# Local attention on one core: mask added by a matmul, one minimum per head, exps from PSUM, and the rotary swap in one instruction

## The chip, the cores and the metric

The kernel runs on one core of a Trainium2 chip. Its engines work side by side, each through its own queue in order: TensorE (PE, with PEld for its weight loads), VectorE (DVE), ScalarE (ACT), GpSimd (POOL) and SyncE (SP, which issues most DMAs). Matmul results land in PSUM, which has eight banks of 128 partitions x 512 float32; other tiles lie in SBUF. The metric is device time of one execution in microseconds, taken as the median of several runs.

## The reference

The program is a chain of four attention layers, each followed by a feed-forward layer, with a residual sum and a layer norm after each, on an input of 4 x 512 rows of 128 numbers as the kernel sees it. The change is in the second of these eight stages, a small transformer of two layers with local attention: 8 heads of 64 numbers, windows of 64 rows, and each row sees its own window up to itself and the window before. Cut to what matters:

```python
q, k = l2norm(q) * qs, l2norm(k) * ksc
q, k = rotary_xpos(q, k)          # q*cos*scale + rotate_half(q)*sin*scale
bq = q.reshape(b, h, w, 64, d) * 8.0
bk, bv = look_around(bk), look_around(bv)      # window before and own: 128 keys
sim = einsum('bhwid,bhwjd->bhwij', bq, bk)
mask = (i < j) | (i > j + 64) | (j == -1)
attn = softmax(where(mask, -max, sim))
out = einsum('bhwij,bhwjd->bhwid', attn, bv)
```

## The kernel before

**Units and heads.** Class F0 holds the stage. A unit u is one layer and one block of 512 rows: two layers x four blocks are 8 units. A unit has 8 heads, taken in 4 pairs, so there are 64 heads and 32 pairs. `run` goes over the heads as items. For each item it writes: the scores of a pair (every second item), `score` of the head, `turn` of the head four items back, and then some steps of the generators that run beside it: `qkv` of the next unit, `values` (the product with V), and `post` of the unit before (projection, layer norm, gated feed-forward).

**What sets the order.** The functions write instructions one after another with a rising priority number. A scheduler then lays out each engine's queue: of the instructions whose inputs and buffers it holds to be ready it takes the one with the lowest number. `k.front()` lowers the number of the score matmuls by 400, so they are laid out as early as their banks allow. `k.waits` adds a wait by hand.

**Scores.** `scores` takes the two PSUM banks with the tag "s", one for each head of the pair. Into each go 16 matmuls of 64 keys' depth: for each window w a 64 x 128 piece (64 query rows, 128 keys). A bank thus holds a head's 512 query rows as four chunks c of 128 rows x 128 keys. The signs in the rotary table make the scores negative, so that the softmax's maximum is a minimum here. There are only two such banks, so the next pair's matmuls cannot start until the readers of this pair are done; the first also waits by hand for `self.emptied`, which is the last reader of the second head.

**Softmax.** In `score`, for each chunk, VectorE adds the mask (`band`, 0 or 1e20) to the scores, multiplies by the inverse norm of the query row (`rn`), writes the result to the SBUF tile `sm` (one buffer) and its row minimum to `nb`, all in one instruction (L1689). ScalarE then reads `sm`, computes exp(nb - sm) into `p`, and gives the row sum to `den` (L1691). `turn` transposes `p` on TensorE (L219) and copies it to `PT` (L1701).

**Rotary.** In `qkv`, for q and k of each chunk, ScalarE copies the projection from PSUM (L1616) and squares it (L1619); VectorE multiplies the swapped halves of each head by the sine table into `tb` (L1623, twice: one instruction for each half), the straight values by the cosine table in place (L1625), and sums the squares (L1626).

**Other names.** L311 to L313 are the three matmuls of a projection in split precision; L1653 scales k by its norm; L343 to L353 are small VectorE steps of an inverse square root; L1726 is the copy of a pair's output; L1333 is a row minimum of another stage (A3), read from a PSUM bank; L1996 and L2117 are ScalarE instructions of other stages, without and with a per-partition scale; L725 is a mask matmul of another stage.

Of the kernel before, what the change touches and what calls it, by code (L numbers as in the profile page):

```python
# [452 lines left out]
class Attn:  # L453
# [4 lines left out]
    nb, lead, lag, ahead = 3, 8, 5, 2  # L458
# [333 lines left out]
class Alibi(Causal):  # L792
    MROW, alibi, nm = 30, True, "a2"
    nb, lead, pre, span = 4, 12, True, "first"
# [18 lines left out]
class Rel(Attn):  # L813
# [4 lines left out]
    nb, lead, lag, ahead = 3, 6, 4, 3  # L818
# [674 lines left out]
class F0:  # L1493
# [83 lines left out]
    def qkv(self, u, X, tag="t"):  # L1577
# [5 lines left out]
        w = self.w  # L1583
# [20 lines left out]
        for c in range(4):  # L1604
            cs = slice(c * P, (c + 1) * P)
            for s in range(3):
                yield from wait()
                ps = k.bank("b")
                ws = slice(512 * s, 512 * s + 512)
                k.mm3(ps, xh[:, cs], xl[:, cs], w["qkvh"][:, ws], w["qkvl"][:, ws])  # L1610
                if s == 2:
                    nc.scalar.copy(v[:, c, :], ps)
                    yield
                    continue
                x = kr[:, c, :] if s else pool.tile([P, 512], F32, tag="ta", name=f"ta{u}{c}", bufs=self.nta)
                nc.scalar.copy(x, ps)  # L1616
                yield
                sq = pool.tile([P, 512], F32, tag="sq", name=f"sq{u}{c}{s}", bufs=1)
                nc.scalar.activation(sq, x, AF.Square)  # L1619
                tb = pool.tile([P, 8, 64], F32, tag="tb", name=f"tb{u}{c}{s}", bufs=2)  # L1620
                x3 = x.rearrange("p (h d) -> p h d", d=64)
                for a, b2 in ((0, 32), (32, 0)):
                    nc.vector.tensor_tensor(tb[:, :, a:a + 32], x3[:, :, b2:b2 + 32],  # L1623
                                            w["tab"][:, 2 * s + 1, c, None, a:a + 32].to_broadcast([P, 8, 32]), ALU.mult)
                nc.vector.tensor_tensor(x3, x3, w["tab"][:, 2 * s, c, None, :].to_broadcast([P, 8, 64]), ALU.mult)  # L1625
                nc.vector.tensor_reduce(ss[:, s, c, :], sq.rearrange("p (h d) -> p h d", d=64), AX.X, ALU.add)  # L1626
# [36 lines left out]
    def scores(self, u, pr):  # L1663


        k, nc = self.k, self.nc
        qT, kT = self.S[u][:2]
        if pr == 0:
            self.den[u] = self.early.tile([P, 4, 8], F32, tag="den", name=f"den{u}", bufs=2)
        self.s = [k.bank("s") for _ in range(2)]  # L1670
        with k.front():
            for w in range(8):
                c, o = w // 2, 64 * (w % 2)
                for e in range(2):
                    r = slice(64 * e, 64 * e + 64)
                    m = nc.tensor.matmul(self.s[e][o:o + 64, c * P:c * P + P], qT[r, pr, 64 * w:64 * w + 64], kT[r, pr, 64 * w:64 * w + P], start=True, stop=True)  # L1676
                    if w == e == 0 and self.emptied:
                        k.waits(m.ins, self.emptied)

    def score(self, u, h):  # L1680

        k, nc, pool = self.k, self.nc, self.pool
        rn, den, s = self.S[u][3], self.den[u], self.s[h % 2]
        p = self.p[8 * u + h] = pool.tile([P, 4, P], F32, tag="p", name=f"p{u}{h}", bufs=self.np)
        nb = pool.tile([P, 4], F32, tag="nb", name=f"nb{u}{h}", bufs=3)
        sm = pool.tile([P, 4, P], F32, tag="sm", name=f"sm{u}{h}", bufs=self.ns)
        for c in range(4):

            m = nc.vector.tensor_tensor_reduce(sm[:, c, :], s[:, c * P:c * P + P], self.band[:, min(c, 1), :],  # L1689
                                           rn[:, 0, c, h:h + 1], 3.0e38, ALU.add, ALU.min, nb[:, c:c + 1])  # L1690
            nc.scalar.activation(p[:, c, :], sm[:, c, :], AF.Exp, bias=nb[:, c:c + 1], scale=-1.0, accum_out=den[:, c, h:h + 1])  # L1691
        self.emptied = m.ins

    def turn(self, u, h):
# [149 lines left out]
    def run(self, Xs):  # L1844
# [4 lines left out]
        self.sel = self.early.tile([P, 4, P], F32R, name="f0sel")  # L1849
        self.lT = k.rows16(self.early, "f0lT")  # L1850
        nc.gpsimd.dma_start(self.sel, k.d["c_sel8"])
        self.v2 = pool.tile([P, 4, 512], F32, name="f0v2")
        nc.gpsimd.memset(self.v2[0:64, 0:1], 0.0)
        self.p, self.emptied = {}, None
# [536 lines left out]
```

## Time and profile before

| | |
|---|---|
| three runs | 2244.31, 2245.49, 2246.03 us; median 2245.49 |
| the profiled execution's own time | 2249.67 us |
| its span, first to last instruction | 2247.6 us |
| mean granted TensorE clock in it | 0.965 |
| stretch in which the attention of the changed stage runs | from 247.7 us (first L1689) to 634.2 us (last L1691) |
| instructions in the span | 43130 |

A profile shows one execution. Busy time is the time in which an engine works; matmuls overlap and their ends are modelled, so a busy TensorE is not one at its peak. A group's row gives line, engine, operation, what it writes and reads, shapes and count; after the first bar stand busy us in all and the mean ns of one; after the second the idle time of the engine just before, and what ended most of it. A wait's row gives who waited for whom: us in all, times, longest. The chain of waits is followed back from the last instruction, at each step to what released it or to the instruction before it on its engine.

### The profile page before, as it was taken

The page shows a single profiled execution, that of the slowest core. Times are in us where ns is not written, and L with a number is a line of the kernel's source. Part 1 is how long each engine was busy: PE and PEld are TensorE (multiplying, and loading weights), DVE is VectorE, ACT ScalarE, POOL GpSimd, SP SyncE. Part 2 cuts the span into 40 slices and gives each one's busy share as a digit, 9 for nine tenths or more (in the row PEclk, how much of TensorE's full clock was granted, in tenths as well). Part 3 has the DMA queues.
Part 4 walks back from the last instruction along what each step waited for, and adds up shares of the span by engine and source line. Part 5 has one row for each costly group of instructions (what it writes and reads, how often), then busy time and mean ns, then how long its engine had stood idle before and what let it go on. Part 6 is the DMA issues. An engine that isn't in the chain of part 4 may idle for free.

```text
span 2247.6 us, 43130 instructions
## 1 busy us (share of the span) xinstructions
PE 2025.6 (90%) x14400; PEld 1472.7 (66%) x14400; DVE 1669.2 (74%) x5592; ACT 1331.7 (59%) x2982; POOL 504.3 (22%) x707
## 2 busy tenths in 40 slices
PE   7999888888878999999999999998999899999897
PEld 4566566676656667676887665776666566666676
DVE  5778688888878676873777775553877877778787
ACT  3566787777734666665333666332877777777632
POOL 3222212111211532433000322531111111111220
PEclk9999999999988999999999999998999999999999
DMA  5321312021433454321021420603889888888400
GB/s 170 106 77 35 102 49 62 8 48 27 116 113 94 143 157 140 113 79 56 16 66 40 117 78 21 218 17 90 209 213 210 203 196 190 195 206 204 104 5 15
DMA packets 264919, 242.10 MB, mean 108 GB/s; under 512 B 106353, under 2 KB 190619, under 8 KB 263867
## 3 DMA queue, kind: packets, MB, share of 16 engines
q1 hardware_dynamic: 259466, 221.86, 37.0%
q0 software_dynamic: 5232, 17.50, 3.3%
q8 instruction: 115, 1.88, 0.4%
q14 instruction: 106, 0.86, 0.1%
HBM read 103.82 MB, written 74.32 MB: 79 GB/s over the span
## 4 chain that ended last, share of the span: by engine, by line
PE 59%; DVE 17%; ACT 9%; DMA 7%; issue 4%; POOL 2%; SPq 1%; ACTq 0%; POOLq 0%; DVEq 0%
PE t L219 5%; PE s L2113 4%; PE o L737 3%; PE s L688 3%; PE t L721 3%; PE o L1377 3%; PE o L1016 3%; PE b L219 3%; PE b L311 3%; PE o L2009 2%; PE s L311 2%; PE b L313 2%; PE b L312 2%; PE s L313 2%; PE s L312 2%
## 5 line engine op out<-in xcount | busy, mean ns | idle before, releaser
L969 DVE CUSTOM_DVE_ANT_0 junk<-w,a1mask 128x640 bf16<-128x640 f32 x256 | 202.9, 817 | 66.3 <-PE w L967 64.4
L219 PE MATMUL t<-ident,p 128*128 128x128 f32 x1280 | 200.6, 278 | 26.4 <-ACT p L1334 17.3
L765 ACT ACTIVATE Pt<-t 128x384 f32<-128x384 f32 (+1 forms) x384 | 179.6, 528 | 67.4 <-PE t L721 55.7
L219 PEld LDWEIGHTS t<-ident,p 128*128 128x128 f32 x1280 | 151.2, 141 | 83.5 <-ACT p L1334 38.3
L1347 ACT COPY PT<-t 128x512 f32<-128x512 f32 x256 | 149.9, 595 | 76.2 <-PE t L219 75.3
L1043 ACT ACTIVATE Pt<-t 128x512 f32<-128x512 f32 x256 | 149.1, 597 | 73.4 <-PE t L1042 44.4
L1334 ACT ACTIVATE p<-s,nb 128x512 f32<-128x512 f32 x256 | 178.2, 700 | 12.4 <-DVE nb L1333 6.7
L1333 DVE TENSOR_REDUCE nb<-s 128x1 f32<-128x512 f32 x256 | 174.4, 685 | 2.5
L690 DVE CUSTOM_DVE_ANT_0 junk<-s,a0mask 128x128 bf16<-128x128 f32 (+3 forms) x256 | 114.1, 484 | 45.9 <-PE s L688 45.0
L1352 DVE CUSTOM_DVE_ANT_0 jk<-p,a3right 128x496 bf16<-128x496 f32 (+3 forms) x256 | 124.6, 487 | 26.9 <-ACT p L1334 14.8
L690 DVE CUSTOM_DVE_ANT_0 junk<-s,a2mask 128x128 bf16<-128x128 f32 (+3 forms) x256 | 114.8, 483 | 30.5 <-PE s L688 30.4
L774 POOL TENSOR_SCALAR_AFFINE_SELECT Pt<-Pt 128x512 f32<-128x512 f32 x112 | 70.0, 637 | 256.4 <-ACT Pt L765 256.3
L1331 DVE TENSOR_TENSOR s<-s,W 128x160 f32<-128x160 f32 (+1 forms) x256 | 80.9, 317 | 62.5 <-PE s L1329 61.2
L1328 PE MATMUL s<-a3KT,a3QT 128*128 128x512 f32 x256 | 118.7, 466 | 5.6 <-DVE nb L1333 2.5
L1377 PE MATMUL o<-PT,V 128*64 128x512 f32 x512 | 116.9, 598 | 0.5 <-ACT PT L1347 0.5
L1691 ACT ACTIVATE p<-sm,nb 128x128 f32<-128x128 f32 x256 | 100.7, 397 | 24.8 <-DVE nb L1689 24.4
L1329 PE MATMUL s<-a3K,a3Q 128*128 128x512 f32 x256 | 102.1, 400 | 0.0
L1040 PE MATMUL t<-a1Q,a1K 128*128 128x512 f32 (+3 forms) x256 | 92.4, 366 | 6.3 <-ACT Pt L1043 3.9
L1689 DVE CUSTOM_DVE_ANT_0 sm<-s,band,rn 128x128 f32<-128x128 f32 x256 | 78.2, 343 | 26.4 <-PE s L1676 19.3
L688 PE MATMUL s<-a0K,a0Q 128*128 128x256 f32 (+2 forms) x256 | 83.8, 387 | 14.4 <-DVE mx L690 7.3
L966 PE MATMUL w<-a1K,a1Q 128*128 128x256 f32 (+2 forms) x192 | 83.1, 433 | 10.6 <-DVE mx L969 9.7
L1996 ACT ACTIVATE sl<-s 128x512 f32<-128x512 f32 x64 | 37.9, 598 | 91.0 <-PE s L313 85.6
(493 smaller groups left out, 5803.3 us busy)
## 6 DMA issues: line engine op xcount, KB each, us to landing
W<-a3dsk SPq DMA_DIRECT2D x32, 640.0 KB
a1Q<-a1iq SPq DMA_DIRECT2D x32, 512.0 KB
a3dpw<-p SPq DMA_DIRECT2D x64, 160.0 KB
a3dpw<-p SPq DMA_DIRECT2D x64, 144.0 KB
a1K<-a1ik SPq DMA_DIRECT2D x64, 128.0 KB
a3Q<-a3dim SPq DMA_DIRECT2D x32, 256.0 KB
a3QT<-H SPq DMA_DIRECT2D x64, 128.0 KB
a3QT<-L SPq DMA_DIRECT2D x64, 128.0 KB
```

Source lines behind the costliest of these rows:

```text
L219: return self.nc.tensor.matmul(out.bitcast(x.dtype), x, i[:n, :n], is_transpose=True, start=start, stop=stop)
L688: self.scored = nc.tensor.matmul(s[:, :nm], self.qof(0, t, i)[:, qc * P:(qc + 1) * P], Ks[:, i, :nm], start=True, stop=True).ins
L690: nc.vector.tensor_tensor_reduce(junk[:, :n], s[:, :n], k.mask[:, 512 - n:512], 1.0, NEG, ALU.add, ALU.max, mx[:, qc, i:i + 1])
L765: ready = nc.scalar.activation(Pt[:, i, z:], s[:, z:], AF.Exp, scale=sc).ins
L969: nc.vector.tensor_tensor_reduce(junk, s.rearrange("p a n -> p (a n)")[:, T - n:T + m], k.mask[:, T - n:T + m], 1.0, NEG, ALU.add, ALU.max ...
L1043: nc.scalar.activation(Pt[:, i, :T], s, AF.Exp, scale=sc)
L1328: nc.tensor.matmul(s, QT[:, e, qs], KT[:, e, :], start=True, stop=False)
L1333: nc.vector.tensor_reduce(nb, s, AX.X, ALU.min)
L1334: nc.scalar.activation(p[:, e, :], s, AF.Exp, bias=nb, scale=-1.0, accum_out=den[:, qc, 2 * un + e:2 * un + e + 1])
L1347: self.copied[t] = nc.scalar.copy(PT[e][:, :, qc * P:qc * P + P], tb.rearrange("p (c n) -> p c n", n=P)).ins
L1352: nc.vector.tensor_tensor_reduce(jk[:, :nn], p[:, e, x0:], w["right"][:, :nn], 1.0, 0.0, ALU.mult, ALU.add, at[:, e, qc, 31:32])
L1377: m = nc.tensor.matmul(o[64 * e:64 * e + 64, :], V[:, kc, h * 64:h * 64 + 64], PT[e][:, kc, :], start=(kc == 0), stop=False)
```

## The change

Four things change. The mask is added inside the scores' bank: a matmul of a bfloat16 identity with a bfloat16 copy of the mask for all four chunks (`band4`) opens each bank, and the score matmuls accumulate on it. VectorE takes the minimum of all four chunks in one reduction over the bank and multiplies the four results by the norm. The exps read the scores from PSUM, with the negated norm (`mrn`, made once per unit) as their scale and the scaled minimum as their bias, so `sm` is gone, and `emptied` is now an exp. Apart from that, the two instructions of the rotary swap become one that walks the halves in reverse. The identity and the mask copies are made once, when the stage starts.

```diff
@@ qkv
-                for a, b2 in ((0, 32), (32, 0)):
-                    nc.vector.tensor_tensor(tb[:, :, a:a + 32], x3[:, :, b2:b2 + 32],
-                                            w["tab"][:, 2 * s + 1, c, None, a:a + 32].to_broadcast([P, 8, 32]), ALU.mult)
+                nc.vector.tensor_tensor(tb.rearrange("p h (a d) -> p h a d", a=2), x.rearrange("p (h a d) -> p h a d", a=2, d=32)[:, :, ::-1],
+                                        w["tab"][:, 2 * s + 1, c].rearrange("p (a d) -> p a d", a=2)[:, None].to_broadcast([P, 8, 2, 32]), ALU.mult)
@@ scores
         if pr == 0:
+            self.mrn = self.pool.tile([P, 4, 8], F32, tag="mrn", name=f"mrn{u}", bufs=2)
+            nc.vector.tensor_scalar(self.mrn, self.S[u][3][:, 0], -1.0, None, ALU.mult)
             self.den[u] = ...
         self.s = [k.bank("s") for _ in range(2)]
         with k.front():
+            for e in range(2):
+                m = nc.tensor.matmul(self.s[e], self.identb, self.band4.rearrange("p c n -> p (c n)"), start=True, stop=False)
+                if e == 0 and self.emptied:
+                    k.waits(m.ins, self.emptied)
             for w in range(8):
                 c, o = w // 2, 64 * (w % 2)
                 for e in range(2):
                     r = slice(64 * e, 64 * e + 64)
-                    m = nc.tensor.matmul(self.s[e][o:o + 64, c * P:c * P + P], qT[...], kT[...], start=True, stop=True)
-                    if w == e == 0 and self.emptied:
-                        k.waits(m.ins, self.emptied)
+                    nc.tensor.matmul(self.s[e][o:o + 64, c * P:c * P + P], qT[...], kT[...], start=False, stop=(w >= 6))
@@ score
-        nb = pool.tile([P, 4], F32, tag="nb", name=f"nb{u}{h}", bufs=3)
-        sm = pool.tile([P, 4, P], F32, tag="sm", name=f"sm{u}{h}", bufs=self.ns)
-        for c in range(4):
-            m = nc.vector.tensor_tensor_reduce(sm[:, c, :], s[:, c * P:c * P + P], self.band[:, min(c, 1), :],
-                                           rn[:, 0, c, h:h + 1], 3.0e38, ALU.add, ALU.min, nb[:, c:c + 1])
-            nc.scalar.activation(p[:, c, :], sm[:, c, :], AF.Exp, bias=nb[:, c:c + 1], scale=-1.0, accum_out=den[:, c, h:h + 1])
+        nb = pool.tile([P, 2, 4], F32, tag="nb", name=f"nb{u}{h}", bufs=3)
+        nc.vector.tensor_reduce(nb[:, 0], s.rearrange("p (c n) -> p c n", n=P), AX.X, ALU.min)
+        nc.vector.tensor_tensor(nb[:, 1], nb[:, 0], rn[:, 0, :, h], ALU.mult)
+        for c in range(4):
+            m = nc.scalar.activation(p[:, c, :], s[:, c * P:c * P + P], AF.Exp, bias=nb[:, 1, c:c + 1], scale=mrn[:, c, h:h + 1],
+                                     accum_out=den[:, c, h:h + 1])
         self.emptied = m.ins
@@ run
+        self.identb = pool.tile([P, P], BF16, name="f0identb")
+        nc.vector.tensor_copy(self.identb, k.ident)
+        self.band4 = pool.tile([P, 4, P], BF16, name="f0band4")
+        nc.vector.tensor_copy(self.band4[:, 0], self.band[:, 0])
+        nc.vector.tensor_copy(self.band4[:, 1:], self.band[:, 1, None].to_broadcast([P, 3, P]))
```

More of the change, by code (lines that the diff above doesn't have):

```diff
@@ L1675, in scores @@
                     r = slice(64 * e, 64 * e + 64)
[L1676 to L1678 removed]
+                    nc.tensor.matmul(self.s[e][o:o + 64, c * P:c * P + P], qT[r, pr, 64 * w:64 * w + 64], kT[r, pr, 64 * w:64 * w + P], start=False, stop=(w >= 6))
     def score(self, u, h):
         k, nc, pool = self.k, self.nc, self.pool
[L1683 removed]
+        rn, mrn, den, s = self.S[u][3], self.mrn, self.den[u], self.s[h % 2]
         p = self.p[8 * u + h] = pool.tile([P, 4, P], F32, tag="p", name=f"p{u}{h}", bufs=self.np)
[L1685 to L1686 removed]
+        nb = pool.tile([P, 2, 4], F32, tag="nb", name=f"nb{u}{h}", bufs=3)
+        nc.vector.tensor_reduce(nb[:, 0], s.rearrange("p (c n) -> p c n", n=P), AX.X, ALU.min)
+        nc.vector.tensor_tensor(nb[:, 1], nb[:, 0], rn[:, 0, :, h], ALU.mult)
         for c in range(4):
[L1689 to L1691 removed]
+            m = nc.scalar.activation(p[:, c, :], s[:, c * P:c * P + P], AF.Exp, bias=nb[:, 1, c:c + 1], scale=mrn[:, c, h:h + 1],
+                                     accum_out=den[:, c, h:h + 1])
         self.emptied = m.ins
```

## The prediction

> **What bounds the kernel now.** I read the page's first part, then cut out the stretch in which the changed lines run (247 to 640 us), and there the busy times, the chain of waits, the groups, the waits and a few rows in order of time.
>
> Over the whole span TensorE looks like the bound:
>
> ```profile
> PE 2025.6 (90%) x14400; PEld 1472.7 (66%) x14400; DVE 1669.2 (74%) x5592; ACT 1331.7 (59%) x2982; POOL 504.3 (22%) x707
> ```
>
> The change touches one stage of eight, so the average says little. The windows view of that stage (us busy, instructions, granted clock):
>
> ```profile
> core 0: us, PE busy (x) PEld busy (x) DVE busy (x) ACT busy (x) POOL busy (x), PEclk, DMA share, GB/s
> 247.00:640.00 393.00, 327.83 (x3511) 256.99 (x3511) 339.96 (x1217) 301.42 (x868) 75.58 (x84) 0.94 0.23 62
> ```
>
> VectorE is the busiest with 87% of 393 us, TensorE follows with 83%, ScalarE with 77%. No engine has much room, and none is alone. The chain of waits in the same window says the same: it goes to and fro among the three.
>
> ```profile
> by line: PE t L219 8.4%; ACT p L1691 7.3%; PE s L1676 5.7%; DVE sm L1689 5.0%; DVE tb L1623 4.7%; PE o L1720 4.6%; issue 4.3%; DVE ss L1626 4.2%; PE b L1759 3.7%; PE b L311 3.7%; PE b L313 3.1%; PE b L1814 2.9%; PE b L312 2.9%; DVE kr L1625
> ...
> ```
>
> Times 393 us, the chain holds 28.7 us of the exps (L1691), 22.4 us of the score matmuls (L1676), 19.7 us of the minima (L1689) and 18.5 us of the rotary swap (L1623). The groups give what these lines cost in all:
>
> ```profile
> L1689 DVE CUSTOM_DVE_ANT_0 sm<-s,band,rn 128x128 f32<-128x128 f32 x256 | 78.2, 343 | 26.4 <-PE s L1676 19.3 <-ACT p L1691 3.9 <-ACT OT L1726 3.0
> L1691 ACT ACTIVATE p<-sm,nb 128x128 f32<-128x128 f32 x256 | 100.7, 397 | 24.8 <-DVE nb L1689 24.4
> L1676 PE MATMUL s<-kT,qT 64*64 64x128 f32 x1010 | 44.1, 294 | 6.3 <-DVE nb L1689 1.7 <-ACT p L1691 1.2 <-DVE rs L343 1.2
> L1623 DVE TENSOR_TENSOR tb<-ta,tab 128x256 f32<-128x256 f32 x56 | 25.2, 486 | 3.8 <-ACT ta L1616 3.5 <-issue 0.3
> L1623 DVE TENSOR_TENSOR tb<-kr,tab 128x256 f32<-128x256 f32 x56 | 21.7, 420 | 1.6 <-ACT kr L1616 1.4
> ```
>
> From these, the share of each line that lies on the path which sets the end: minima 19.7 of 79.2 us (busy with their readouts, windows view of that line) = 0.25; swap 18.5 of 46.9 = 0.39; exps 28.7 of 119.0 (with readouts, same view) = 0.24; score matmuls 22.4 of 44.1 = 0.51. A saved or added microsecond counts by that share, as long as the chain keeps its shape.
>
> **The change part by part.** *Minima.* Four instructions per head, 64 heads, now 79.2 us. Afterwards one reduction 128x4 from a 128x512 bank and one 128x4 product. A3's own minimum reads the same width from the same memory, and the small product is like L348 (128x4: 156 ns):
>
> ```profile
> L1333 DVE TENSOR_REDUCE nb<-s 128x1 f32<-128x512 f32 x256 | 174.4, 685 | 2.5
> ```
>
> 64 x (0.685 + 0.156) = 53.8 us, so VectorE does 25.4 us less; times 0.25 = -6.3. Bounds: 0 if the four-part result makes it slow, -25.4 if VectorE were the path throughout.
>
> *Swap.* Two 128x256 products become one 128x512; L1625, the same operation unsplit, takes 700 and 683 ns (L1653 682). 56 x 0.70 = 39.2 against 46.9 us: -7.7, times 0.39 = -3.0. No row walks backwards; I take the forward price since every run is still 32 contiguous elements, and keep double price as the other end (below). The scaled copy mrn is 8 x 0.156 us and the setup casts about 1 us before the attention starts: +0.4 on the path.
>
> *Exps.* They gain a second per-partition operand (scale beside bias) and read PSUM. Rows for a second operand, same shape, PSUM input, without and with an operand for the scale:
>
> ```profile
> L1996 ACT ACTIVATE sl<-s 128x512 f32<-128x512 f32 x64 | 37.9, 598 | 91.0 <-PE s L313 85.6 <-DVE acc L2013 3.5 <-DVE a2va L676 1.7
> L2117 ACT ACTIVATE h<-s,f2s 128x512 f32<-128x512 f32 x16 | 11.0, 689 | 27.9 <-PE s L2113 26.9 <-POOL hhl L2076 1.0
> ```
>
> +91 ns. SBUF input (L1619, 634) against PSUM (L1996, 598) gives back up to 36 ns. So between +55 and +91 ns, or nothing if it vanishes in the overlap of back-to-back exps; I take +70, nearest to rows that differ by the operand alone: 256 x 0.070 = +18 us on ScalarE, times 0.24 = +4.3.
>
> *Masks on TensorE.* Two 512-column one-pass matmuls per pair of heads, 32 pairs. The nearest rows are the projections' one-pass matmuls (start, duration):
>
> ```profile
> 401.01 0.50 PE L311 MATMUL b<-wqkv1h,f0xh 128*128 128x512 f32 x1
> 401.35 0.40 PE L312 MATMUL b<-wqkv1h,f0xl 128*128 128x512 f32 x1
> 401.58 0.40 PE L313 MATMUL b<-wqkv1l,f0xh 128*128 128x512 f32 x1
> 401.81 0.39 PE L311 MATMUL b<-wqkv1h,f0xh 128*128 128x512 f32 x1
> ```
>
> One starts 0.23 us after another: 64 x 0.23 = 14.7 us, times 0.51 = +7.5. Their weight loads I cost at nothing: in this trace the full-array load of L312 starts at 401.12, while L311's full-array matmul runs until 401.51. A rule of the Trainium skill (TensorE: Matmul & The Clock Gate, "The mechanism") speaks against that: a load overlaps matmuls in flight only where its row group is another. By it 64 loads of 96 ns (L725's are that long) would be bare, 6 us more TensorE time and 3 more in the sum; the trace shows the overlap, so the sum goes by the trace.
>
> *Where exps start.* Rows of one head now (L1689 is the minimum of one quarter, L1691 its exp):
>
> ```profile
> 412.87 0.34 DVE L1689 CUSTOM_DVE_ANT_0 sm<-s,band,rn 128x128 f32<-128x128 f32 x1
> ...
> 413.25 0.40 ACT L1691 ACTIVATE p<-sm,nb 128x128 f32<-128x128 f32 x1 [3.05 <-DVE nb L1689]
> ...
> 413.65 0.39 ACT L1691 ACTIVATE p<-sm,nb 128x128 f32<-128x128 f32 x1
> ```
>
> The first exp starts 0.38 us after the minimum does, pipelined by quarters. Afterwards it waits for the whole head: 0.685 + 0.156 + 0.03 = 0.87, later by 0.49 us. ScalarE waits on that hand-over 22 times:
>
> ```profile
> ACT p L1691 <- DVE nb L1689: 24.4, 22, 3.0
> ...
> DVE sm L1689 <- ACT p L1691: 3.9, 5, 1.1
> DVE sm L1689 <- ACT OT L1726: 3.0, 2, 2.3
> ...
> PEld s L1676 <- DVE nb L1689: 2.2, 7, 0.6
> ```
>
> 22 x 0.49 x 0.24 = +2.6. The two middle rows are waits for the single masked copy sm, which goes: -6.9 x 0.25 = -1.7.
>
> *When the bank is handed over.* This is the added wait. Now VectorE alone reads the scores, and the next pair's matmuls wait for the second head's last minimum; afterwards for its last exp. From the start of that head's minimum it was 1.16 us (412.87 to 414.03); it becomes 0.87 + 4 x 0.455 (now 0.385 apart, plus 0.070) = 2.7, later by 1.5 us. Behind the waiting matmul all of TensorE's queue stands: transposes, values, projections. TensorE waits there now 9 times (7 loads above, 2 matmuls at L1676). In 27 of the 31 changes of pair the matmuls start within 1.3 us of the last minimum (counted in the rows in order of time), in 25 before the last exp has ended, so the queue is laid out for the early release. I take half of the 9 as covered by transposes and projections that a new layout puts ahead: 9 x 1.5 x 0.5 x 0.51 = +3.4; without that cover +6.9, with every pair waiting +24.
>
> Sum: -6.3 - 3.0 + 0.4 + 4.3 + 7.5 + 2.6 - 1.7 + 3.4 = +7.2 us. On the profiled execution's own 2249.67 us (span 2247.6) that is 2256.9; the median of the runs, 2245.49, lies 4.2 lower, so 2252.7.
>
> **The rivals.** *VectorE sets the pace (faster).* The chain's shares assume that its shape stays. VectorE has the most busy time, and the change takes 25.4 + 7.7 - 1.3 = 31.8 us off it (340 to 308) while ScalarE goes to 319 and TensorE to 343. If VectorE's 53 idle us stay as they are, the stage falls by all 31.8. But TensorE's 343 plus those of its present 65 idle us that VectorE does not end (it ends some 24: ta, kr, rs, h, xTl and lnv in the list of waits; 41 are left) are 384, which allows only 9. Between them, about -16: 2229. For it: L1689 and L1623 are 126 us of the busiest engine. Against: they hold only 38 us of the chain. It decides where TensorE's stalls after the change are mostly under 40 us in this stage.
>
> *The bank hand-over locks the pairs (slower by more).* All 31 changes of pair wait the 1.5 us: 24 in place of 3.4, so +28: 2273. It decides once more than some 18 pairs show the wait.
>
> *The reversed walk is slow, so the swap is no gain.* At double price 56 x 1.36 = 76 us against 46.9: +11 in place of -3.0, so +21: 2267.
>
> *It cancels.* Work only changes place: -33 on VectorE, +18 and +15 on the others. Each term could be off by a few us, and the sum then falls within 4.5 us of the median.
>
> **How the numbers follow.** 0.2% (4.5 us) is about what a measurement of this kernel can tell from no change. Chances: my sum, slower by 4.5 to 16 us, 0.36; hand-over lock 0.09; slow reversed walk 0.04; together slower 0.49. VectorE as pacer 0.36 faster; cancelling 0.15. Predicted 2252.7, the likeliest case's own range 2250 to 2262. Cases of both signs hold most of the chance, so the range takes in the pacer's middle and a little beyond (2224) and the lock (2275); outside are the full -31.8 and a lock joined by a slow walk.
>
> **What would show it.** In the stage's window: VectorE busy near 308, ScalarE 319, TensorE 343; a wide minimum of about 0.69 us; swaps of 0.70; exps of about 0.46 us; a row of score matmuls or band loads waiting for L1691's exps more than 9 times, and ScalarE's wait for nb growing. I am wrong if the stage ends over 5 us sooner with VectorE's idle time no greater: then the chain's shares misled, and busy time was the better guide.

## The result and the profile after

The changed kernel takes 2280.58 us (median of five runs, 2278.25 to 2288.72) against 2245.12 us for the kernel before (five runs beside them): a ratio of 1.0164, 95% interval 1.0143 to 1.0186, or +36 us. The forecast was 2252.7 us with a range of 2224 to 2275. The sign was right, the size was five times too small, and the time lies outside the range. The profiled execution of the changed kernel is the longest of its five, 2288.72 us with a span of 2287.0 us (before: 2247.6), so some 8 us of what its profile shows belong to this execution alone.

The time is lost in the stage that was edited. From the start of the first exp to the end of the last (rows in order of time) it was 386.5 us before and is 432.3 us now, +45.8; the stage starts 4 us later, and the rest of the span after it is 11 us shorter (1613.1 to 1602.3). Windows view of the changed kernel's stage, with its column names:

```profile
core 0: us, PE busy (x) PEld busy (x) DVE busy (x) ACT busy (x) POOL busy (x), PEclk, DMA share, GB/s
247.00:682.00 435.00, 360.16 (x3550) 271.90 (x3546) 311.81 (x780) 314.58 (x855) 74.86 (x81) 0.90 0.21 54
```

Set against the window of before (327.83, 339.96 and 301.42 us in 393 us), VectorE has done what was asked of it: 28 us less. ScalarE has 13 us more, TensorE 32 us more at a granted clock of 0.90 in place of 0.94. (Forecast were 308, 319 and 343 us for VectorE, ScalarE and TensorE; TensorE alone is far off.) Cut exactly from first exp to last exp, the three are busy for 357.2, 309.9 and 315.1 us (before 323.9, 335.9 and 298.0). All three now have more idle time than before; none of them fills the stage. Of ScalarE's 17 us more (315.1 against 298.0), 5 are four more loads of a function table. ScalarE loads a table where it changes between the exps and the two Gelu activations of each unit's feed-forward (L1800, now L1803), once each way. Before, the two Gelus of each of the six units in the stage stand together, six visits; now exps lie between them in two of the six, eight visits:

```profile
L1800 ACT ACT_TABLE_LOAD x6 | 7.7, 1283 | 0.1
L1691 ACT ACT_TABLE_LOAD x6 | 7.7, 1283 | 0.1
```

```profile
L1803 ACT ACT_TABLE_LOAD x8 | 10.3, 1283 | 0.1
L1693 ACT ACT_TABLE_LOAD x8 | 10.3, 1283 | 2.1 <-DVE nb L1691 2.0
```

The granted clock may have a part too. Among the five executions of the changed kernel the time goes with it: 2278.25 us at a mean of 0.963, 2288.72 us at 0.954. At that rate the 0.006 between the usual 0.965 of before and 0.959 now would be some 7 of the 36 us, an estimate. Whether the clock is lower because TensorE waits more, no run here separates.

The chain of waits in the window of 247 to 682 us names the lines that the stage's time goes through:

```profile
by line: ACT p L1693 13.3%; PE t L219 7.1%; PE s L1681 5.3%; PE o L1723 5.0%; PE b L1762 3.5%; PE b L311 3.4%; issue 3.2%; DVE nb L1690 3.2%; PE b L312 3.1%; DVE tb L1622 3.0%; DVE ss L1625 3.0%; PE b L1817 2.8%; PE b L313 2.7%; ACT sq L161
```

The exps (now L1693) hold 13.3% of 435 us, 57.9 us, and lead the list. Before it was 28.7 us. Their groups, with the other new lines, by form:

```profile
L1693 ACT ACTIVATE p<-s,nb,mrn 128x128 f32<-128x128 f32 x256 | 114.5, 466 | 20.4 <-DVE nb L1691 19.8
...
L1690 DVE TENSOR_REDUCE nb<-s 128x4 f32<-128x512 f32 x64 | 42.5, 682 | 11.2 <-PE s L1681 11.1
...
L1674 PE MATMUL s<-f0band,f0identb 128*128 128x512 bf16 x64 | 23.6, 451 | 12.5 <-ACT p L1693 12.4
...
L1622 DVE TENSOR_TENSOR tb<-ta,tab 128x512 f32<-128x512 f32 x28 | 20.3, 725 | 15.2 <-ACT ta L1616 13.3 <-PE t L219 1.0 <-POOL kr L1632 0.8
...
L1622 DVE TENSOR_TENSOR tb<-kr,tab 128x512 f32<-128x512 f32 x28 | 20.0, 713 | 4.8 <-ACT kr L1616 4.8
```

The single durations came out nearly as forecast: the wide minimum 682 ns (forecast 685), the one-instruction swap 725 and 713 (700), the exps 466 (397 + 70 = 467). What moved is who waits (us, times, longest):

```profile
ACT p L1693 <- DVE nb L1691: 19.8, 16, 4.3
...
PEld L1674 <- ACT p L1693: 18.5, 18, 3.7
...
DVE ta L1624 <- ACT sq L1619: 15.9, 12, 3.4
...
PE s L1674 <- ACT p L1693: 12.4, 12, 3.2
...
DVE nb L1690 <- PE s L1681: 11.1, 8, 2.8
```

TensorE now waits for exps in front of the mask matmul (L1674) in 18 of the 31 changes of pair, for 18.5 us by its weight loads. The 12 waits in the matmuls' row (PE) lie in the same changes, some 10 ns later, and don't add to them. In the kernel before, the 9 waits on the minima (7 of loads, 2 of matmuls) belong to 8 changes of pair, 3.6 us. Rows in order of time show one such change of pair (start, duration):

```profile
414.66 1.29 DVE L1690 TENSOR_REDUCE nb<-s 128x4 f32<-128x512 f32 x2
...
417.73 0.48 ACT L1693 ACTIVATE p<-s,nb,mrn 128x128 f32<-128x128 f32 x1
...
418.17 0.65 ACT L1619 ACTIVATE sq<-ta 128x512 f32<-128x512 f32 x1
...
418.69 0.48 ACT L1693 ACTIVATE p<-s,nb,mrn 128x128 f32<-128x128 f32 x1
...
419.99 0.50 ACT L1693 ACTIVATE p<-s,nb,mrn 128x128 f32<-128x128 f32 x1
...
420.59 0.27 PE L219 MATMUL t<-ident,p 128*128 128x128 f32 x1
420.63 0.17 PEld L1674 LDWEIGHTS <-f0identb 128*128 128x128 bf16 x2
420.70 0.59 PE L1674 MATMUL s<-f0band,f0identb 128*128 128x512 bf16 x2
```

Both minima of a pair are done within 1.29 us from 414.66. The exps of the first head (the last of them is the row at 417.73) begin only when ScalarE has finished other work, then come a square of the projections (L1619) and four exps of the second head. The next pair's mask load follows 0.14 us after the last exp's end (419.99 + 0.50). The bank was read for the last time by VectorE at about 415.95, and is handed over at 420.6.

### The profile page after: what moved, and what is told of

Read it like the earlier page. It is cut to its first block, busy times and chain, and to the rows that moved or that the text cites. A ratio compares the mean times of both kernels' runs of the same rounds, so it can differ in the third digit from the quotient of the medians.

```text
span 2287.0 us, 42785 instructions
## 1 busy us (share of the span) xinstructions
PE 2065.9 (90%) x14464; PEld 1494.5 (65%) x14464; DVE 1637.5 (72%) x5155; ACT 1351.2 (59%) x2986; POOL 506.7 (22%) x707
## 4 chain that ended last, share of the span: by engine, by line
PE 60%; DVE 17%; ACT 11%; DMA 5%; issue 4%; POOL 2%; SPq 1%; ACTq 0%; POOLq 0%; DVEq 0%
PE t L219 5%; PE s L2121 4%; PE o L1377 4%; PE o L737 3%; PE t L721 3%; PE s L688 3%; PE o L1016 3%; PE b L219 3%; ACT p L1693 3%; PE o L2017 2%; PE b L311 2%; PE s L311 2%; PE b L312 2%; PE b L313 2%; PE s L313 2%
## 5 line engine op out<-in xcount | busy, mean ns | idle before, releaser
L219 PE MATMUL t<-ident,p 128*128 128x128 f32 x1280 | 205.7, 280 | 23.0 <-ACT p L1334 12.7
L219 PEld LDWEIGHTS t<-ident,p 128*128 128x128 f32 x1280 | 152.0, 142 | 85.2 <-ACT p L1334 35.1
L1693 ACT ACTIVATE p<-s,nb,mrn 128x128 f32<-128x128 f32 x256 | 114.5, 466 | 20.4 <-DVE nb L1691 19.8
L967 PE MATMUL w<-a1K,a1Q 128*128 128x512 f32 (+3 forms) x256 | 87.7, 344 | 0.0
```

The costliest lines, as they stand in the source:

```text
L219: return self.nc.tensor.matmul(out.bitcast(x.dtype), x, i[:n, :n], is_transpose=True, start=start, stop=stop)
L1693: m = nc.scalar.activation(p[:, c, :], s[:, c * P:c * P + P], AF.Exp, bias=nb[:, 1, c:c + 1], scale=mrn[:, c, h:h + 1], accum_out=den[:, c ...
```

## The experiments

Two theories were set against each other after the first runs. **D**: the stage is paced by ScalarE's total time, wherever it is added. **E**: the exps count because of their place, since they now hold the score banks until their end (a ring of minimum, product, eight exps and release). **F**, added at the end: several things stand level in the kernel before, so that an addition on one engine counts and a removal on one engine does not. The quoted expectations weigh the theories as they stood when each run was made: the first ones set theory A (the late hand-over of the banks is the loss) against the rivals B (the moved work adds up) and C (the reversed walk is slow); rival L, later, is that any new order of the queues costs. a1, a2, a3, c2, b1 and b2 leave out part of the computation (the mask, the norm, or the squares of k), so they serve to compare times only.

All runs, each with its ratio to the kernel before on the same chip; the stage is cut from first to last exp in the profiled execution, and "tables" are the loads of a function table (ACT_TABLE_LOAD) in it:

| kernel | us | ratio, 95% | stage us | PE / DVE / ACT busy in it | tables |
|---|---|---|---|---|---|
| before | 2245.12 | | 386.5 | 323.9 / 335.9 / 298.0 | 12 |
| changed | 2280.58 | 1.0164 [1.0143, 1.0186] | 432.3 | 357.2 / 309.9 / 315.1 | 16 |
| e1_rotary | 2245.17 | 0.9989 [0.9974, 1.0003] | 383.5 | 324.5 / 329.4 / 298.5 | 12 |
| e2_wait | 2259.17 | 1.0055 [1.0033, 1.0077] | 400.7 | 331.6 / 338.4 / 304.5 | 16 |
| e3_band | 2267.60 | 1.0087 [1.0061, 1.0114] | 407.9 | 339.0 / 334.9 / 304.6 | 18 |
| e4_scale | 2276.03 | 1.0130 [1.0105, 1.0156] | 416.1 | 334.4 / 338.7 / 326.5 | 16 |
| d1_wait_scale | 2272.96 | 1.0101 [1.0066, 1.0136] | 413.3 | 341.0 / 336.0 / 323.5 | 14 |
| c1_other | 2272.84 | 1.0121 [1.0104, 1.0139] | 412.7 | 334.5 / 334.8 / 326.7 | 18 |
| b2_before_noksq | 2242.02 | 0.9978 [0.9962, 0.9993] | 383.5 | 326.2 / 335.0 / 283.8 | 12 |
| v1_ksq | 2262.15 | 1.0067 [1.0044, 1.0089] | 399.4 | 328.0 / 345.4 / 284.6 | 12 |
| a1_no_mask | 2284.39 | 1.0159 [1.0132, 1.0187] | 427.4 | 343.0 / 313.7 / 322.1 | 20 |
| a2_const_scale | 2246.47 | 1.0001 [0.9983, 1.0019] | 388.6 | 337.7 / 312.5 / 284.0 | 12 |
| a3_neither | 2253.77 | 1.0028 [1.0012, 1.0045] | 390.9 | 330.3 / 314.8 / 287.0 | 12 |
| c2_a2_other | 2261.30 | 1.0067 [1.0052, 1.0082] | 396.1 | 338.6 / 310.0 / 304.6 | 12 |
| b1_after_noksq | 2280.73 | 1.0151 [1.0127, 1.0175] | 423.0 | 351.9 / 316.7 / 298.9 | 16 |
| e5_after3 | 2300.16 | 1.0228 [1.0199, 1.0256] | 432.7 | 377.4 / 318.0 / 310.3 | 12 |
| e6_before3 | 2301.61 | 1.0241 [1.0210, 1.0272] | 438.1 | 378.2 / 336.3 / 307.6 | 16 |
| n1_tile | 2248.00 | 0.9991 [0.9976, 1.0006] | 386.5 | 323.7 / 335.6 / 298.2 | 12 |
| n2_swap | 2244.77 | 0.9991 [0.9976, 1.0006] | 385.5 | 323.9 / 336.0 / 298.3 | 12 |
| n4_wait | 2248.70 | 1.0010 [0.9991, 1.0028] | 387.1 | 326.0 / 335.4 / 298.9 | 12 |

### One edit at a time on the kernel before: e1, e2, e3, e4

e1, the swap alone:

```diff
-                for a, b2 in ((0, 32), (32, 0)):
-                    nc.vector.tensor_tensor(tb[:, :, a:a + 32], x3[:, :, b2:b2 + 32], ...)
+                nc.vector.tensor_tensor(tb..., x.rearrange("p (h a d) -> p h a d", a=2, d=32)[:, :, ::-1], ...)
```

> The kernel before with the one-instruction rotary swap alone. Theory A (the loss is the bank hand-over: the score banks are held until the last exp, and TensorE's queue stands behind that wait): the swap has no part in it, VectorE does some 7 us less, the time falls by 0 to 4 us. Rival B (the loss is the sum of the moved work: TensorE +23 us, ScalarE +17 us of busy time): the same, 0 to 4 us faster. Rival C (the reversed walk makes the swap slow): slower by 5 us or more, with the swap over 0.84 us.

e2, the late hand-over alone; `m` becomes the last exp, so that `emptied` is an exp and the next pair's first score matmul waits for it:

```diff
-            nc.scalar.activation(p[:, c, :], sm[:, c, :], AF.Exp, ...)
+            m = nc.scalar.activation(p[:, c, :], sm[:, c, :], AF.Exp, ...)
```

> The kernel before, where the first score matmul of a pair waits for the second head's last exp in place of its last minimum; nothing else is changed, all work is as before. Theory A: this wait alone costs most of the loss, +20 to +35 us, and the scores start right after the last exp in most of the 31 changes of pair. Rival B: the work is unchanged, so within 5 us of before.

e3, the mask matmuls alone, VectorE adding the mask as before:

```diff
         with k.front():
+            for e in range(2):
+                m = nc.tensor.matmul(self.s[e], self.identb, self.band4..., start=True, stop=False)
...
-                    m = nc.tensor.matmul(..., start=True, stop=True)
+                    nc.tensor.matmul(..., start=False, stop=(w >= 6))
```

> The kernel before with the two mask matmuls per pair ahead of the scores; VectorE goes on adding the mask (masked scores get it twice, and their exps are 0 either way) and releases the banks as before. Theory A: TensorE's added work costs +4 to +9 us. Rival B: TensorE's work is the larger half of the loss, +12 to +25 us.

e4, the second operand alone; the exps read SBUF as before, and their scale of -1 comes from a column of a tile:

```diff
-            nc.scalar.activation(p[:, c, :], sm[:, c, :], AF.Exp, bias=nb[:, c:c + 1], scale=-1.0, ...)
+            nc.scalar.activation(p[:, c, :], sm[:, c, :], AF.Exp, bias=nb[:, c:c + 1], scale=self.neg, ...)
```

> The kernel before with the exps' scale of -1 read from a per-partition tile in place of a constant; all else as before. Theory A: each exp is longer by 0.09 us (0.397 to 0.49), 256 of them 23 us of ScalarE, which cost +3 to +8 us. Rival B: +10 to +18 us.

The swap takes 2.5 us off (0.9989; the interval just reaches 1). Its groups in e1 show no slow walk:

```profile
L1622 DVE TENSOR_TENSOR tb<-ta,tab 128x512 f32<-128x512 f32 x28 | 21.4, 763 | 3.0 <-ACT ta L1616 2.7 <-issue 0.3
...
L1622 DVE TENSOR_TENSOR tb<-kr,tab 128x512 f32<-128x512 f32 x28 | 19.4, 693 | 2.8 <-ACT kr L1616 2.7
```

The late hand-over costs 12 us (between theory A's 20 to 35 and rival B's 5), the masks 20 (in B's range), the scale operand 29 (above both). Four, six and four more table loads, 5.1, 7.7 and 5.1 us of ScalarE's time, are in these prices, so neither the hand-over nor the masks were priced quite alone. The exps' group in e4, beside 397 ns before:

```profile
L1691 ACT ACTIVATE p<-sm,nb,f0neg 128x128 f32<-128x128 f32 x256 | 124.3, 489 | 24.6 <-DVE nb L1689 24.1
```

92 ns more on each of 256 exps. In the rows, the starts of exps that follow one another directly lie 479 ns apart, before 386: +93 ns, so nothing vanishes in the overlap, and 256 x 0.093 = 23.8 us. With four more table loads of 1.283 us that is 28.9, and ScalarE is in fact busy for 28.5 us more. The stage grew by 29.6 us: a microsecond added on an engine with 88 idle us in the stage cost a whole one. The single costs sum to 59, more than the 36 of the whole change; but the whole also has the wide minimum and the exps' PSUM input, which no run has alone, so this doesn't show that the costs fail to add (d1 below does).

### The changed kernel without a part: a1, a2, a3

a1 leaves out the two mask matmuls of each pair, and with them the mask; a2 takes the operand away, and with it the norm (its exps also no longer wait for the product with the norm, one small VectorE instruction):

```diff
-            m = nc.scalar.activation(p[:, c, :], s[...], AF.Exp, bias=nb[:, 1, c:c + 1], scale=mrn[:, c, h:h + 1],
+            m = nc.scalar.activation(p[:, c, :], s[...], AF.Exp, bias=nb[:, 0, c:c + 1], scale=-1.0,
```

a3 does both.

> The changed kernel without the two mask matmuls per pair (the mask is left out of the scores, the score matmuls open the bank themselves); minima, exps and the bank's release as changed. Theory D: the 23.6 us of mask matmuls come back, 15 to 24 us faster than the changed kernel, +12 to +22 us against before. Theory A (the hand-over of the banks alone is the loss): up to 5 us faster than the changed kernel, +31 us or more against before.

> The changed kernel with exps that take the constant scale -1 and the unscaled minimum as bias (the norm is left out of the exps); the products with the norm and all else stay. Theory D: exps fall from 0.466 to some 0.38 us, 22 us of ScalarE come back, 18 to 27 us faster than the changed kernel, +9 to +19 us against before. Theory A: the bank is held 0.7 us per pair less, 5 to 12 us faster than the changed kernel.

> The changed kernel without the mask matmuls (mask left out) and with the constant scale and the unscaled minimum as bias (norm left out of the exps): what stays of the change is the wide minimum, the product, the swap and the bank's release by the exps. Theory D: VectorE's relief of 33 us against the wait's +12 us, 5 to 20 us faster than before. If the wait is what holds the stage: within 5 us of before, like the run with the constant scale alone.

Without the masks nothing is won (1.0159 against 1.0164, 1 ± 8 us), though a1 has four more table loads, 5 us, than the changed kernel. Without the operand the whole loss is gone: 1.0001, 37 us where theory D had forecast 18 to 27 and A 5 to 12. Since ScalarE's wait for the minimum is about the same in a2 (18.0 us, 19.8 in the changed kernel), the shorter way to the exps accounts for little of that by itself. Its exps, and their share of the chain (8.6% of 393 us, 33.8 us):

```profile
L1693 ACT ACTIVATE p<-s,nb 128x128 f32<-128x128 f32 x256 | 93.1, 391 | 18.3 <-DVE nb L1690 18.0
```

```profile
by line: ACT p L1693 8.6%; PE t L219 7.0%; PE s L1681 6.3%; PE o L1723 5.2%; issue 3.9%; PE b L1817 3.7%; PE b L311 3.6%; PE b L1762 3.4%; DVE tb L1622 3.0%; PE b L312 3.0%; DVE ss L1625 2.9%; PE b L313 2.8%; DVE kr L1652 2.7%; PE b L219 2.
```

The starts of its exps lie 342 ns apart, in the changed kernel 435: again +93 ns, 23.8 us in all. (342 against the 386 of before: reading PSUM in place of SBUF saves 44 ns on each exp.) The four steps close a square. From before to a3 (swap, wide minimum, late hand-over, exps from PSUM) +6 us; the operand then adds 29 us (a3 to a1), the masks 1 (a1 to the changed kernel). The other way round, everything but the operand costs nothing (a2), and the operand then adds 37 us (difference of the ratios 0.0163, about ± 0.0028, times 2245). By either way it carries some four fifths of the loss or more. ScalarE's time in the stage grows by more than the operand's 23.8 us on both ways, by 35.1 us from a3 to a1 and 31.1 from a2 to the changed kernel, since eight and four table loads come with it. Per microsecond of ScalarE's time the price is 0.8 and 1.2.

The hand-over's waits are there in a2 as well:

```profile
PEld L1674 <- ACT p L1693: 11.4, 14, 2.3
...
PE s L1674 <- ACT p L1693: 6.0, 8, 1.8
```

All of these lie in 14 changes of pair: 11.4 us at no loss against before. That the matmuls wait for the exps is thus not enough by itself to make the kernel slower.

### Where the added ScalarE time lies: c1 and c2

Both give a scale operand, of 1, to 256 other ScalarE instructions (copies of `ta`, `kr`, `v`, `qT`, `kT`, `PT`, `OT`, each now an Identity with that scale); c1 on the kernel before, c2 on a2:

```diff
-        self.copied = nc.scalar.copy(PT, t).ins
+        self.copied = nc.scalar.activation(PT, t, AF.Identity, scale=self.one).ins
...
```

> The kernel before with a per-partition scale of 1 on 256 other ScalarE instructions of the stage (the PSUM copies of q, k, v, their transposes, the transposed exps and the outputs, 0.58 us each); the exps keep their constant. As many instructions and as many added microseconds (23) as in the run that gave the exps the operand and cost +29 us. Theory D (any ScalarE time in the stage counts): +18 to +32 us. Theory E (only the exps count, because minimum, exps and the release of the one buffer or bank follow each other from head to head): 0 to +10 us.

> The changed kernel with short exps (constant scale, unscaled minimum as bias; the norm is left out of the exps, the time was that of before) and with the per-partition scale of 1 on the same 256 other ScalarE instructions: ScalarE's work is again that of the changed kernel, but not in the exps. Theory D: the loss is back, +25 to +45 us against before. Theory E: 0 to +12 us against before.

On the kernel before it costs 27 us for 28.7 us of ScalarE's time (7.7 of them six more table loads), as much as e4's, with the exps untouched at 396 ns:

```profile
L1693 ACT ACTIVATE p<-sm,nb 128x128 f32<-128x128 f32 x256 | 100.4, 396 | 18.1 <-DVE nb L1691 17.3
...
L1703 ACT ACTIVATE PT<-t,f0one 128x512 f32<-128x512 f32 x64 | 43.2, 681 | 3.8 <-PE t L219 3.5
```

There theory D holds, and the exps' place is not needed for the price. On a2 it costs 15 us (0.0066 ± 0.0023), between the forecasts of D (25 to 45) and E (0 to 12), for 20.6 us of ScalarE's time with no more table loads, where the exps' operand costs 37 us for 31.1. Per microsecond that is 0.7 ± 0.25 against 1.2 ± 0.2. The exps' place may make the difference, but so may the granted clock: over the whole execution it is 0.967 in a2 and c2 and 0.959 in the changed kernel, and at the rate given with the result this would be some 9 of the 37 us, which leaves 0.9. That the exps' place costs something extra is therefore not shown; that ScalarE work elsewhere costs too, and per microsecond more than half as much, is.

### Taking ScalarE time away: b1, b2, v1

b1 (on the changed kernel) and b2 (on the kernel before) leave out the 32 squares of k, some 16 us of ScalarE outside the exps; v1 gives them to GpSimd on e1.

```diff
-                nc.scalar.activation(sq, x, AF.Square)
+                if s == 0:                  # b1, b2
+                    nc.scalar.activation(sq, x, AF.Square)
...
+                if s:                       # v1
+                    nc.gpsimd.tensor_tensor(sq, x, x, ALU.mult)
```

> The changed kernel without the 32 squares of k (k is scaled by q's norm in place of its own): 20 us of ScalarE go from outside the exps, VectorE's sums stay. Theory D: 18 to 32 us faster than the changed kernel, +5 to +19 us against before. Theory E: 0 to 8 us faster than the changed kernel.

> Kernel before, with the 32 squares of k on ScalarE left out (k is then scaled by q's norm); about 16 to 20 us less ScalarE time in the stage, outside the exps. The other runs showed that ScalarE time added to the kernel before costs about 1 us for each us. Theory D (ScalarE's time paces the kernel before): removed time comes back at the same rate, 2245 - 14 to -20 = 2225 to 2231. Theory F (several engines and buffers stand level at about 386 us: additions count, a removal on one engine alone does not): 2241 to 2249, and the stage stays at 383 to 388 us.

> The kernel before with the one-instruction swap, and with the squares of k (32 of the 64 Square instructions, 0.63 us each) made by GpSimd in place of ScalarE: 20 us of ScalarE go, 41 us of GpSimd come, and GpSimd is busy for 75 of 393 us only. Theory D with ScalarE as the engine whose time counts: 12 to 22 us faster than before. Rival L: slower, as any new order is. A third possibility: VectorE's sum waits for the slower square and its own instructions are drawn out beside GpSimd's, 0 to 10 us slower.

Removal is not addition reversed. b2 gives 5 us (0.0022 ± 0.0016) for 14.2 us less ScalarE time, and its stage stays at 383.5 us: theory F. b1 gives 3 ± 7 us for 16.2 us less, within theory E's 0 to 8. TensorE's waits for the exps in b1 have grown from 18.5 to 28.7 us (loads), in 19 changes of pair in place of 18, so part of what ScalarE saved shows again as waiting; why is not shown:

```profile
PEld L1675 <- ACT p L1694: 28.7, 19, 5.1
PE s L1675 <- ACT p L1694: 23.0, 11, 4.9
```

v1 misses what D forecast and lies beyond the third possibility's 10 us; L's plain "slower" fits it, but the controls below speak against L. ScalarE's time falls as wanted, but the kernel slows by 15 us, and VectorE is drawn out from 329 us in e1 to 345. Two groups in v1, GpSimd's squares and VectorE's swap of k:

```profile
L1620 POOL TENSOR_TENSOR sq<-kr 128x512 f32<-128x512 f32 x28 | 35.6, 1271 | 115.3 <-DVE ss L1628 62.0 <-ACT kr L1616 33.3 <-ACT p L1693 7.0
...
L1625 DVE TENSOR_TENSOR tb<-kr,tab 128x512 f32<-128x512 f32 x28 | 28.2, 1006 | 2.4 <-ACT kr L1616 2.2
```

### Do hand-over and operand feed each other: d1

d1 joins the edits of e2 and e4 on the kernel before.

> Kernel before, with both of two single edits: the next pair's first score matmul waits for the last exp (alone +12 us), and the exps' scale is a per-partition operand of -1 (alone +29 us). If the two costs merely add: 2245 + 41 = 2286. If the longer exps lengthen what the matmuls now wait for (theory E: hand-over and exps' length feed each other): more, 2290 to 2300. If both use the same idle time: 2270 to 2279.

+23 us (± 8), less than 12 + 29 and no more than e4 alone. The two don't feed each other in the kernel before, and here they don't add; that the second edit uses idle time which the first has made fits, but isn't shown. TensorE waits there in 11 changes of pair for 8.8 us (five of the six waits of matmuls lie beside one of a load), half of what the changed kernel shows:

```profile
PEld s L1676 <- ACT p L1691: 7.9, 10, 3.0
...
PE s L1676 <- ACT p L1691: 6.1, 6, 2.6
```

### A third score bank: e5 and e6

PSUM has eight banks; a third score bank has to come from the projections. e5 does that on the changed kernel, e6 on the kernel before, both without the wait by hand:

```diff
-    banks = dict(s=2, t=2, o=1, b=3)
+    banks = dict(s=3, t=2, o=1, b=2)
```

> The changed kernel with three score banks in place of two (and two projection banks in place of three), and without the hand-made wait: the next pair's first bank is free at once, its second after the first head's exps. Theory A: the loss is mostly gone, 20 us or more faster than the changed kernel, within 15 us of before. Theory D: the work is the same, only the 12 us that the wait alone cost can come back, and fewer projection banks may cost some: +20 to +40 us against before.

> The control for the run with three score banks: the kernel before with three score banks, two projection banks and no hand-made wait. If the lost projection bank is what made that run +51 us, this one is +25 us or more as well, and the third score bank's own worth to the changed kernel is the difference; if this one is within 8 us of before, a score bank that is free at once does not help the changed kernel, and theory A (the hand-over of the banks alone) falls with it.

Each is slower than its parent, and e5, 51 us above before, misses what both theories forecast for it. The projections' missing bank costs the kernel before 54 us, so e5 is read against e6: 0.0013 ± 0.0042 below it. With a third score bank the changed kernel thus costs nothing more than the old one. That fits theory E (the hold of the bank is what makes the longer exps dear). But both now run at a TensorE busy time of 377 us, and e6 at a lower granted clock over the execution (0.950, e5 0.959), so another limit may merely hide the operand. It doesn't settle the question.

### Controls on the order: n1, n2, n4

The scheduler lays out every queue anew when anything is edited. n1 adds an unused tile of one column, n2 exchanges two independent VectorE instructions, n4 lowers a delay of the generators by one step (`wait_rn` 7 for 8), all on the kernel before.

> The kernel before with one more 128x1 tile, set once and read by nobody, as in the run with the per-partition scale; the exps keep their constant. The first four runs alone cost +12 (wait), +20 (mask matmuls), +29 (scale operand), -2 (swap). Theory D (in this stage nearly every microsecond that ScalarE or TensorE gets counts in full, whatever the chain's shares say): no work is added, within 4 us of before. Rival L (the order of the queues before is a lucky one, and any other order that the scheduler lays out costs 10 to 25 us): +8 to +25 us.

> The kernel before with two independent VectorE instructions of the rotary step written in the other order (the sum of squares ahead of the cosine product); the work is the same to the instruction, but the scheduler lays the queues out anew (336 lines of ScalarE's order differ). Theory D (added engine time counts): within 5 us of before. Rival L (any new order costs): +8 to +25 us.

> The kernel before with one pause less in the generator that prepares the next unit (7 in place of 8 pauses between the norm and its use); the work is the same, the order of the queues is another from before the stage on. Theory D: within 5 us of before. Rival L: +8 to +25 us.

They move the time by -0.09, -0.09 and +0.10%, within the error. None of these new orders makes 1.6%; all three keep the 12 table loads. The slower kernels with 14 to 20 loads have orders in which exps come between the two Gelus of a unit, seven to ten visits in place of six.

## Why the prediction was wrong

**The step that failed is the exps' term: "+70 ... 256 x 0.070 = +18 us on ScalarE, times 0.24 = +4.3".** Not the duration: 466 ns came where 467 were forecast. Start to start, it is 93 ns for the operand less 44 ns for the PSUM input. (The Trainium skill, "ScalarE: Activation LUTs", section "What ACT_TABLE_LOAD costs", has about 93 ns for each per-partition pointer operand; the runs agree.) What failed is the price, the share of the chain. (The 119.0 us under that share also hold the six table loads of L1691, 7.7 us; without them it is 0.26, which moves the term by 0.3 us only.) The operand alone cost 29 us (e4), and taken from the changed kernel it gave back 37 (a2) or 29 (a1 to a3): 1.2 to 1.5 us for each of its 23.8 us, or 0.8 to 1.2 for each microsecond that ScalarE is then in fact busier (table loads among them), not 0.24. The chain followed back from the last instruction says how much of a line lies on one path. It doesn't say how close the next path is. Work added elsewhere on ScalarE cost as much (c1), so the price isn't a matter of the exps' own share; that a next path lies so close because each engine waits for each of the others is the likely reason, argued and not shown. The share itself grows: 28.7 us of exps in the chain before, 44.5 in e4 (10.7% of 416), 57.9 after. The sentence "as long as the chain keeps its shape" was the condition, and it failed.

**The right sign is partly luck.** The largest plus in the sum of +7.2 is the masks' +7.5, and a1 shows about nothing for them in the changed kernel; without it the sum is -0.3.

**The shares did better for cuts than for additions, as far as the error allows.** Swap: -3.0 forecast, -2.5 ± 3 measured. ScalarE's squares: b2 gave back 0.35 ± 0.25 us for each removed. Minima: from before to a3 is +6; e1 and e2 by themselves explain -2.5 + 12, which leaves some -3 for the wide minimum and the PSUM input (which takes 256 x 0.044 = 11 us off ScalarE), where -6.3 was forecast for the minimum. This is a difference of four runs and good to some 7 us.

**Masks, +7.5.** Wrong in both directions: alone they cost 20 us (e3), in the changed kernel about nothing (a1; between a3 and a2 -6 ± 5). Their TensorE time was forecast well (14.7 us; a1 has 14.2 us less busy time). In the change of pair shown above their load starts at 420.63, while a full-array transpose is shown until 420.86, so in that row too a load overlaps a matmul (ends are modelled). The other 19 us of TensorE's additional busy time were not forecast; the clock of 0.90 in place of 0.94 would stretch 324 us by some 14, an estimate. In e3 six more table loads, 7.7 us, are in the 20; in a1 four more, 5.1 us, may hide as much of a gain. That TensorE has room for the masks where the banks wait for exps anyway is argued, not shown.

**Later start and hand-over, +2.6, +3.4 and -1.7.** The hand-over alone costs 12 us, 5 of which may be its four more table loads. "ScalarE's wait for nb growing" was wrong: it fell from 24.4 to 19.8 us (22 times to 16). In the change of pair shown, ScalarE is busy with something else when the minimum arrives.

**The rivals.** The hand-over lock stands just at its own sign: it "decides once more than some 18 pairs show the wait", and 18 of 31 do, for 18.5 us in all. (The prediction, too, counted loads and matmuls together: its 9 waits are 8 changes of pair.) But a2 has 14 of them without a loss and is 37 us faster, so its mechanism doesn't carry the time without the longer exps; how much of the 37 us is due to the hold and how much to ScalarE's time as such stays open, with 15 of 37 (c2) as the part that ScalarE work elsewhere would cost too, at 20.6 in place of 31.1 us, and some 9 that may go with the clock. VectorE as the pacer fell: VectorE's busy time dropped by 26.0 us and the stage grew; in a2 and a3, with 23 and 21 us of the relief, it doesn't shrink. The slow reversed walk fell (725 ns). That it cancels is true of everything but the operand (a2).

**The range** failed with the price. The exps' term had bounds of +55 and +91 ns and none on the share, so that its largest value was 23.3 x 0.24 = 5.6 us. With a share of 1 for ScalarE's and TensorE's additions as the upper bound (23.3 for 4.3 and 14.7 for 7.5 in the sum) it would have reached 2279, close to the result, but in part by luck, since a1 finds no price for the masks there.

**Left open.** Why the masks cost 20 us alone, beyond their loads; what part the granted clock has as cause or as consequence; what holds the stage at about 386 us, where b2, e1, a2 and a3 all end (383.5 to 390.9 us) with VectorE between 312 and 335 us and ScalarE between 284 and 299. None of the versions beats the kernel before beyond doubt: e1 lies within the error, and b2 computes less.

## What to carry to other kernels

In a stage where three engines are 77 to 87% busy and hand work to and fro, price additions on ScalarE at a whole microsecond for each, and cuts with caution at their share of the chain: both signs were measured here on that engine only (c1 and e4 at about 1, c2 at 0.7, b2 at 0.35). TensorE's masks cost more than their time alone and about nothing in the changed kernel. Count the table loads of the new order as well, since they are ScalarE time that no line of the edit shows. Before folding a factor into an activation as its per-partition scale, count the instructions: here 93 ns each cost more than both VectorE savings brought. And when a consumer moves to reading PSUM itself, its length becomes part of the time the bank is held; a copy that looks like waste (`sm`) may be what frees the bank early.

## What the runs showed of the hardware

- A second per-partition operand adds 93 ns to an exp of 128x128 start to start, from SBUF (386 to 479) and from PSUM (342 to 435) alike. It is not hidden in the overlap of back-to-back instructions. A 128x512 copy made an Identity with a scale operand took 102 ns longer (`PT`, 579 to 681; what the operand and the function each add was not separated).
- Reading PSUM in place of SBUF shortens the distance of such exps by 44 ns, though the single duration falls by only 6 (397 to 391): in such a run the spacing, not the duration, is what each exp costs.
- The reversed walk over 32-element runs costs VectorE little or nothing: 763 and 693 ns in e1 (725 and 713 in the changed kernel), against two halves of 486 and 420 ns each, and 700 and 683 for the straight product.
- With squares of 128x512 on GpSimd (1271 ns each), VectorE's swap of k went from 693 to 1006 ns.
- TensorE's granted clock in the stage is lower in most of the slower kernels, not in all: 0.94 before and in a2, 0.92 in e4 and c1, 0.90 after, 0.88 in e6 (with the same matmuls as before), but 0.95 in c2, which is 15 us slower.
- A change between exps and Gelu cost ScalarE one table load of 1283 ns each way; how often depends on the order of the queue: 12 to 20 loads in the stage.
